# Two attention layers on one core: score tiles in three double banks, two of which are lent to the other products between groups of scores

## The chip, the core and the metric

The kernel runs on one core of a Trainium2 chip. The metric is the device time of one launch in microseconds; lower is better. The engines named here are TensorE (PE, matrix products; its weight loads have a row of their own, PEld), VectorE (DVE), ScalarE (ACT), GpSimd (POOL) and SyncE (SP, which issues DMAs). TensorE writes its results into PSUM, which this kernel divides into eight banks, each holding 512 fp32 values for every one of the 128 partitions. All data is fp32.

## The reference

Four images of 32x32 tokens and 768 channels go through two attention layers, each with a group norm before it and a residual around it.

```python
# layer 0 (12 heads of 64)
x = x + proj(softmax(q k^T / 8 + rel_h(q) + rel_w(q)) v)      # q, k, v = gn(x) @ W + b
# layer 1
q, k, v = layer_norm(dwconv3x3(gn(x) @ w_qkv.T + b_qkv))        # per head
x = x + proj(softmax(q k^T / 8 + rel_h(q) + rel_w(q)) v + q)
```

`rel_h` and `rel_w` are position biases that are made from q itself: one term for the key's row, one for the key's column. In layer 0 the bias of v can be added after the softmax, because the weights of the softmax sum to one.

## The kernel before

The work is cut into 8 stages (an image in a layer; images 0 and 1 in layer 0, the same two in layer 1, then images 2 and 3 in the same way), and each stage into 6 pairs of heads: 48 pairs in all. `attend` runs one pair. For each half of the queries (512, two halves) and for each group of four blocks of 128 keys it makes four score tiles, so there are 192 groups and 768 score tiles. A score tile is 128 keys by 2 heads by 512 queries and fills two banks. TensorE makes it from q and k (line 669) and adds the position bias (line 671); ACT takes its exponential into SBUF (line 676). After the four score tiles of a group come further products, then the four products with v (line 690), which add up in one bank, `av`; DVE adds the exponentials for the softmax's denominator (lines 682 and 684).

Everything else is woven in. `attend` yields four times per group, and each yield is a step; a table `events` says which pieces of other work are issued at which step: the q, k and v products of the next pair (`product`, `plain_v`, and in layer 0 `sevens`, which makes four products of halves out of seven), the convolution on DVE (`taps`), its layer norm (`centre`, `squares`, `norm`, `back`), the position products (`positions`), the group norm of the next stage, and the output projection of the last stage (`project`). The order on TensorE, DVE, ACT and GpSimd is the order in which the program issues; nothing reorders it. So an instruction that waits holds back all that follows on its engine.

Steps 0 and 1 stand between the first group's scores and its products with v, steps 2 and 3 after those products, steps 4 to 7 the same for the second group, steps 8 to 15 for the second half of the queries.

PSUM: `ps_s` holds two score tiles (four banks), `ps_av` one bank, and `ps_m` three banks, which all other products take in turn (`bank`). A tile can be written anew once the last reader of the tile that had its place is done. So the third score tile of a group waits for the exponential of the first, and the fourth for that of the second.

The softmax's denominator is finished late: `attend` leaves two pieces, `sums` (product `z`, line 639, and the reciprocal on ACT) and `result` (four instructions on DVE), in the list `rest`, and `more()`, called after the scores and after the products with v of each group, issues one of them.

In layer 0 the bias of v enters in `project`: for image 0, each of six output blocks gets six products of one column (`pbias`, line 713), which turn the bias of v into a bias of the output. Layer 1 does the same with the bias of its layer norm. `mix_tokens` (line 234) makes in five DVE instructions the sums of token halves that `sevens` reads.

Of the kernel before, what the change touches and what calls it, by code (L numbers as in the profile page):

```python
# [9 lines left out]
F32 = mybir.dt.float32  # L10
# [7 lines left out]
P = 128  # L18
# [7 lines left out]
QC = 512  # L26
# [19 lines left out]
def two_layers(ctx: ExitStack, tc: tile.TileContext, keep, x_in, wqkv, wproj, rels, windows, vrow, small, const, onehot, picks, out):  # L46
# [25 lines left out]
    work = pool("work", 2)  # L72
    one = pool("one", 1)
    stat = pool("stat", 3)
    ps_s = pool("ps_s", 2, space=PSUM)
    ps_av = pool("ps_av", 1, space=PSUM)
    ps_m = pool("ps_m", 3, space=PSUM)

    def bank(name):
        return ps_m.tile([P, 512], F32, tag="bank", name=name)  # L80

    def halves(ps, a, b, start=True, stop=True, **kw):

# [153 lines left out]
    def group_norm(stage):  # L237

        xn = xns[stage]
        st = stat.tile([P, NC * 2, 6], F32, tag="bn", name="bn", bufs=1)  # L240
        for n in range(NC):
            for h in range(2):
                nc.vector.bn_stats(st[:, 2 * n + h, :], xn[:, n, h * HALF : (h + 1) * HALF])
            if n in (1, 3):
                yield
        mv = stat.tile([P, 2], F32, tag="mv", name="mv")
        nc.vector.bn_aggr(mv, st.rearrange("p a b -> p (a b)"))
        yield
        yield
        group = cst[:, GROUP : GROUP + P]  # L250
        ps = bank("gn_mean")
        nc.tensor.matmul(ps[:, 0:1], group, mv[:, 0:1], start=True, stop=True)
        mean = stat.tile([P, 1], F32, tag="gmean", name="gmean")
        nc.vector.tensor_copy(mean, ps[:, 0:1])
        d = stat.tile([P, 1], F32, tag="gd", name="gd")
        nc.vector.tensor_sub(d, mv[:, 0:1], mean)
        nc.vector.scalar_tensor_tensor(d, d, d, mv[:, 1:2], ALU.mult, ALU.add)
        yield
        yield
        ps = bank("gn_var")  # L260
        nc.tensor.matmul(ps[:, 0:1], group, d, start=True, stop=True)
        v = stat.tile([P, 1], F32, tag="gv", name="gv")
        nc.vector.tensor_scalar(v, ps[:, 0:1], EPS, None, ALU.add)
        yield
        r = rsqrt(v, 1, "gn")
        yield
        for n in range(NC):
            nc.vector.tensor_scalar(xn[:, n, :], xn[:, n, :], mean, r, ALU.subtract, ALU.mult)  # L268
            if n % 2:
                yield  # L270
# [7 lines left out]
    sk = fixed.tile([P, NSMALL], F32, tag="sk", name="sk")  # L278
    nc.vector.tensor_scalar(sk, sm, SCALE, None, ALU.mult)

    pbias = fixed.tile([P, 2, NC], F32, tag="pbias", name="pbias")

    ones = fixed.tile([P, T], F32R, tag="ones", name="ones")
    plain = one.tile([P, T], F32, tag="whole", name="plain")
# [8 lines left out]
    class Pair:  # L293
# [15 lines left out]
        def sevens(self, s, second):  # L309

            xn = xns[self.b, self.layer]
            x11, x12, x21, x22 = (xn[:, n : n + 3, h : h + HALF] for n in (0, 3) for h in (0, HALF))

            def m(ps, at, x, more=False):

                w = weights[self.i, s, at // 2][:, 3 * (at % 2) : 3 * (at % 2) + 3, :]  # L320
                for t in range(4 if s else 1):
                    for n in range(3):
                        flags = dict(start=not (t or n or more), stop=n == 2, skip_group_check=True)
                        if s:
                            tokens = slice(t * P, (t + 1) * P)
                            halves(ps[:, tokens], x[:, n, tokens], w[:, n, :], **flags)
                        else:
                            halves(ps, w[:, n, :], x[:, n, :], **flags)

            add = lambda to, x, y, op=ALU.add: nc.vector.tensor_tensor(to, x, y, op)  # L330
            u, w = terms
            if not second:
                self.banks = b1, b2 = bank("m4m2"), bank("m3m5")
                m(b1, 0, x21)
                nc.scalar.copy(u, b1)
                m(b2, 1, x12)
                used((self.i, s, 0))
                add(u, u, b2)
                m(b1, 2, x11, more=True)
                add(w, u, b1, ALU.subtract)  # L340
                self.put(s, 1, 0, b1)
                m(b2, 3, x22, more=True)
                used((self.i, s, 1))
                add(u, u, b2, ALU.subtract)
                self.put(s, 0, 1, b2)
            else:
                b3, b4 = bank("m1m6"), bank("m7")
                m(b3, 4, quarters[0])
                add(u, u, b3)
                m(b4, 5, quarters[2])  # L350
                used((self.i, s, 2))
                self.put(s, 0, 0, b4, u)
                m(b3, 6, quarters[1], more=True)
                used((self.i, s, 3))
                self.put(s, 1, 1, b3, w)
# [258 lines left out]
    def attend(pair, os):  # L614
# [7 lines left out]
        def more():  # L622
            nonlocal found
            if rest:
                found = rest.pop(0)(*found)

        for c in range(T // QC):
# [6 lines left out]

            def sums(weighed, acc, c=c):

                z = bank("z")
                for j in range(2):
                    nc.tensor.matmul(  # L639
                        z[j * D : (j + 1) * D, :], cst[:, ONES : ONES + D], acc[:, j, :],  # L640
                        start=True, stop=True,
                    )
                at = 2 * (pair.i * (T // QC) + c)
                t = work.tile([P, QC], F32, tag="t", name="t", bufs=1)
                inv = work.tile([P, QC], F32, tag="inv", name="inv", bufs=1)
                nc.scalar.activation(t, z, AF.Copy, accum_out=seen[:, at : at + 1])

                nc.scalar.activation(inv, t, AF.Ln, bias=tiny)
                nc.scalar.activation(inv, inv, AF.Exp, scale=-1.0, accum_out=seen[:, at + 1 : at + 2])
                return weighed, t, inv  # L650

            def result(weighed, t, inv, cols=cols):

                nc.vector.scalar_tensor_tensor(t, t, -1.0, inv, ALU.mult, ALU.mult)
                nc.vector.scalar_tensor_tensor(inv, t, 2.0, inv, ALU.add, ALU.mult)

                if pair.layer:
                    nc.vector.tensor_tensor(inv, weighed, inv, ALU.mult)
                    nc.vector.scalar_tensor_tensor(q[:, cols], inv, col(LN + 4), q[:, cols], ALU.mult, ALU.add)
                else:  # L660
                    nc.vector.tensor_tensor(q[:, cols], weighed, inv, ALU.mult)

            for g in range(0, NKT, 4):
                es = []
                for kt in range(g, g + 4):
                    keys = slice(kt * P, (kt + 1) * P)
                    ps = ps_s.tile([P, 2, QC], F32, tag="s", name="s")
                    for j, rows in enumerate(heads):
                        nc.tensor.matmul(ps[:, j, :], k[rows, keys], q[rows, cols], start=True, stop=False)  # L669
                    for j, rows in enumerate(heads):  # L670
                        nc.tensor.matmul(  # L671
                            ps[:, j, :], ones[rows, keys], bias[c][rows, kt // 2, :],
                            start=False, stop=True,
                        )
                    e = work.tile([P, 2, QC], F32, tag="e", name="e", bufs=4)
                    nc.scalar.activation(e, ps, AF.Exp)  # L676
                    es.append(e)
                more()
                if g == 0:
                    av = ps_av.tile([P, QC], F32, tag="av", name="av")  # L680
# [6 lines left out]
                for t, e in enumerate(es):  # L687
                    kt = g + t
                    for j in range(2):
                        nc.tensor.matmul(  # L690
                            av[j * D : (j + 1) * D, :], pair.vt[:, kt, j * D : (j + 1) * D], e[:, j, :],
                            start=(kt == 0), stop=(kt == NKT - 1),
                        )
                more()
                if g + 4 == NKT:
                    rest.extend((sums, result))
                    found = (copy(av), acc)
                yield
                yield
# [1 line left out]
    def project(stage, os):  # L701
# [3 lines left out]
        for m in range(NC):  # L705
            w = wp.tile([P, NC, P], F32, tag="wproj", name="wproj_t")
            nc.sync.dma_start(w, wproj[layer, :, :, m, :].rearrange("h p q -> p h q"))
            bias = col(BIAS[layer] + 18 + m)
            if b == 0:
                ps = bank("pbias")  # L710
                for n in range(NC):
                    v_bias = col(LN + 5) if layer else col(BIAS[0] + 12 + n)
                    nc.tensor.matmul(ps[:, 0:1], w[:, n, :], v_bias, start=(n == 0), stop=(n == NC - 1))
                nc.vector.tensor_tensor(pbias[:, layer, m : m + 1], ps[:, 0:1], bias, ALU.add)
            bias = pbias[:, layer, m : m + 1]
            for h in range(2):
                cols = slice(h * HALF, (h + 1) * HALF)
                x = wp.tile([P, HALF], F32, tag="x", name="x")
# [16 lines left out]
    for k in range(1, len(stages)):  # L735
# [5 lines left out]
        if stages[k][1] == 0:  # L741
            mix = mix_tokens(stages[k])
            for r in range(5):
                at(first + 5 * n_steps + r - (0 if stages[k - 1][1] else 8), lambda mix=mix: next(mix, None))
        elif stages[k - 1][1] == 0:
            at(first + 4 * n_steps + 6, lambda: [nc.gpsimd.memset(pad, 0.0) for pad in pads])
    mix = mix_tokens(stages[0])
# [29 lines left out]
    def check():  # L777
# [2 lines left out]
        nc.vector.tensor_reduce(total, seen, AX.X, ALU.add)  # L780
        good = stat.tile([P, 1], F32, tag="good", name="good")
        nc.vector.tensor_scalar(good, total, LIMIT, None, ALU.is_lt)
        ps = bank("good")
        nc.tensor.matmul(ps[:1, :1], cst[:, ONES : ONES + 1], good, start=True, stop=True)
        bad = keep.tile([1, 1], mybir.dt.int32, tag="bad", name="bad")
        nc.vector.tensor_scalar(bad, ps[:1, :1], -1.0, 1.0 * P, ALU.mult, ALU.add)
# [5 lines left out]
    bad = check()  # L792
    for piece in last[2:]:
        piece()
    return bad
@with_exitstack
def general(ctx: ExitStack, tc: tile.TileContext, bad, x_in, wqkv, wproj, rels, windows, vrow, small, const, onehot, picks, out):
# [286 lines left out]
```

## Time and profile before

| what | value |
|---|---|
| median of 3 runs (lowest to highest) | 4041.1 us (4039.57 to 4045.22) |
| the profiled execution | 4040.44 us, its span 4038.7 us, granted TensorE clock 0.996 |
| busy: PE, PEld, DVE, ACT, POOL | 98%, 43%, 62%, 45%, 10% |
| chain that ended last, PE's share | 85% |
| PE's first matmul starts, last one ends | 15.3 us, 4032.9 us after the span's start |

Busy time of an engine counts from an instruction's start to its end as the profile models it. Matmuls overlap in the pipeline, so a busy TensorE can still be late: what a wait costs is read from the distance between starts. Waits are listed with the one that waited, what ended the wait, the sum in us, how often, and the longest.

### The profile page before, as it was taken

The numbers are of one execution on the slowest core, as the hardware profiler recorded it, in microseconds if no ns is written. First come the engines' busy times: TensorE is split into PE (matmuls) and PEld (weight loads), VectorE is DVE, ScalarE is ACT, GpSimd is POOL, SyncE is SP. The second block draws the span as 40 slices with busy tenths as digits, with TensorE's granted clock in tenths as the row PEclk, the third lists the DMA queues.
The fourth block names the chain that finished last, engine by engine and source line by source line (L and its number), as shares of the span: only waits on it lengthen the run. The fifth ranks groups of instructions, "written<-read, shape, count | busy, mean of one in ns | idle before, by whom it ended". The sixth has DMA issues, their size and how long they took to land.

```text
span 4038.7 us, 79929 instructions
## 1 busy us (share of the span) xinstructions
PE 3945.2 (98%) x35098; PEld 1720.3 (43%) x35098; DVE 2494.3 (62%) x2800; ACT 1812.1 (45%) x2669; POOL 409.8 (10%) x776
## 2 busy tenths in 40 slices
PE   7999999999999999999899999999999999999999
PEld 3534444434344444444444344354343444434443
DVE  2455423558489985799633454245575898848883
ACT  2444424545255553455423544244443555525552
POOL 0111100110000110010011110001100011000010
PEclk9999999999999999999999999999999999999999
DMA  5333242221411222212133222422114112131112
GB/s 160 85 112 113 71 128 73 57 65 38 132 48 38 76 52 75 63 49 69 41 103 88 58 70 63 144 58 70 47 53 127 37 43 53 40 104 43 38 47 75
DMA packets 179046, 293.34 MB, mean 73 GB/s; under 512 B 22528, under 2 KB 77952, under 8 KB 178688
## 3 DMA queue, kind: packets, MB, share of 16 engines
q1 hardware_dynamic: 117248, 187.41, 14.8%
q0 software_dynamic: 61440, 100.71, 10.9%
q8 instruction: 279, 4.57, 0.5%
q14 instruction: 79, 0.65, 0.1%
HBM read 153.36 MB, written 34.01 MB: 46 GB/s over the span
## 4 chain that ended last, share of the span: by engine, by line
PE 85%; DVE 8%; ACT 3%; issue 1%; DMA 1%; POOL 0%; DVEq 0%; SPq 0%; ACTq 0%
PE qkv L85 18%; PE av L690 14%; PE s L669 14%; PE proj L85 12%; PE m3m L85 4%; PE m4m L85 4%; PE m1m L85 4%; PE s L671 3%; PE ln_c L85 3%; PE rel L517 3%; PE z L639 2%; DVE shared L459 2%; DVE acc L684 2%; PE m L85 2%; ACT e L676 2%
## 5 line engine op out<-in xcount | busy, mean ns | idle before, releaser
L676 ACT ACTIVATE e<-s 128x1024 f32<-128x1024 f32 x768 | 781.3, 1023 | 529.8 <-PE s L671 503.7
L669 PE MATMUL s<-q,k 64*128 64x512 f32 x3072 | 831.8, 618 | 27.9 <-ACT e L676 22.2
L684 DVE TENSOR_TENSOR acc<-acc,e 128x1024 f32<-128x1024 f32 x576 | 705.4, 1225 | 184.4 <-ACT e L676 133.4
L85 PE MATMUL qkv<-xn,wqkv_t 128*64 128x512 f32 x3648 | 815.6, 596 | 2.8 <-DVE xn L268 2.6
L459 DVE SCALAR_TENSOR_TENSOR shared<-shared,sm 128x1056 f32<-128x1056 f32 x576 | 758.3, 1316 | 14.9
L671 PE MATMUL s<-bias,ones 64*128 64x512 f32 x1536 | 615.6, 794 | 13.9 <-DMA bias<-whole 9.5
L690 PE MATMUL av<-e,vt 128*64 128x512 f32 x2624 | 594.5, 595 | 0.0
L544 POOL DMA_DIRECT2D bias<-high x384 | 204.1, 552 | 3356.5 <-ACT high L533 3097.9
L85 PE MATMUL proj<-q,wproj_t 128*64 128x512 f32 x2304 | 504.9, 593 | 0.0
L85 PEld LDWEIGHTS qkv<-xn,wqkv_t 128*64 128x64 f32 x3648 | 252.9, 137 | 488.5 <-issue 482.6
L669 PEld LDWEIGHTS s<-q,k 64*128 64x128 f32 x3072 | 255.4, 186 | 362.0 <-ACT e L676 210.6
L442 ACT ACTIVATE shared<-qkv,sm 128x512 f32<-128x512 f32 (+1 forms) x288 | 129.2, 501 | 595.6 <-PE qkv L85 595.6
L723 DVE SCALAR_TENSOR_TENSOR x<-proj,pbias,x 128x512 f32<-128x512 f32 x96 | 72.1, 751 | 439.4 <-PE proj L85 435.0
L690 PEld LDWEIGHTS av<-e,vt 128*64 128x64 f32 x2624 | 184.7, 137 | 347.5 <-issue 328.9
L682 DVE TENSOR_TENSOR acc<-e 128x1024 f32<-128x1024 f32 x96 | 117.6, 1225 | 345.4 <-ACT e L676 344.6
L85 PEld LDWEIGHTS proj<-q,wproj_t 128*64 128x64 f32 x2304 | 163.7, 137 | 313.5 <-issue 311.7
L671 PEld LDWEIGHTS s<-bias,ones 64*128 64x128 f32 x1536 | 150.2, 188 | 199.6 <-issue 193.6
L544 POOL DMA_DIRECT2D bias<-whole x384 | 204.9, 562 | 119.5 <-DVE whole L534 109.0
L632 ACT COPY weighed<-av 128x512 f32<-128x512 f32 x96 | 56.3, 586 | 329.2 <-PE av L690 329.2
L85 PEld LDWEIGHTS ln_c<-cst,shared 128*64 128x64 f32 x2304 | 131.4, 138 | 44.4 <-issue 34.6
L517 PEld LDWEIGHTS rel<-q,rel 64*32 64x32 f32 x6144 | 111.6, 105 | 78.0 <-issue 61.0
L85 PE MATMUL ln_c<-cst,shared 128*64 128x128 f32 x2304 | 139.2, 274 | 3.1 <-DVE shared L459 3.1
(119 smaller groups left out, 3613.0 us busy)
## 6 DMA issues: line engine op xcount, KB each, us to landing
bias<-high POOLq DMA_DIRECT2D x384, 128.0 KB, 2.8
bias<-whole POOLq DMA_DIRECT2D x384, 128.0 KB, 3.0
wqkv_t<-in_wqkv SPq DMA_DIRECT2D x78, 384.0 KB, 3.1
wqkv_t<-mixed SPq DMA_DIRECT2D x66, 384.0 KB, 3.1
wproj_t<-in_wproj SPq DMA_DIRECT2D x48, 384.0 KB, 3.7
wqkv_t<-in_wqkv SPq DMA_DIRECT2D x66, 192.0 KB, 2.5
xn<-in_x SPq DMA_DIRECT2D x24, 512.0 KB, 7.8
x<-in_x SPq DMA_DIRECT2D x48, 256.0 KB, 2.8
```

The source lines that it names most:

```text
L85: nc.tensor.matmul(ps[lo : lo + D], a[:, lo : lo + D], b, start=start, stop=stop, **kw)
L442: nc.scalar.activation(self.pad[s][:, rows, there : there + src.shape[2]], src, AF.Identity, bias=col(self.column(s)))
L459: nc.vector.scalar_tensor_tensor(y, window, tap, y, ALU.mult, ALU.add)
L517: nc.tensor.matmul(ps[lo : lo + S, k * S : (k + 1) * S].rearrange("p (b c) -> p b c", b=2), rel[rows, 2 * self.layer + i, first : first + ...
L544: nc.gpsimd.dma_start(sets, some.unsqueeze(1).to_broadcast([D // 2, 2, QC]))
L639: nc.tensor.matmul(z[j * D : (j + 1) * D, :], cst[:, ONES : ONES + D], acc[:, j, :], start=True, stop=True,)
L669: nc.tensor.matmul(ps[:, j, :], k[rows, keys], q[rows, cols], start=True, stop=False)
L671: nc.tensor.matmul(ps[:, j, :], ones[rows, keys], bias[c][rows, kt // 2, :], start=False, stop=True,)
L676: nc.scalar.activation(e, ps, AF.Exp)
L682: nc.vector.tensor_tensor(acc, es[0], es[1], ALU.add)
L684: nc.vector.tensor_tensor(acc, acc, e, ALU.add)
L690: nc.tensor.matmul(av[j * D : (j + 1) * D, :], pair.vt[:, kt, j * D : (j + 1) * D], e[:, j, :], start=(kt == 0), stop=(kt == NKT - 1),)
```

## The change

- PSUM is divided otherwise. `ps_a` holds one score tile (two banks, bank 0 and 1), `ps_av` one bank, `ps_small` one bank, and two places, `place_b` and `place_c`, have two banks each. A place can be opened as a pair (one score tile) or as two single banks; each opening closes the pool that was there. The four score tiles of a group go to a, b, c and a.
- The other products take single banks: two from one place, then two from the other. `other_work` sets which place comes first: b after the scores, c after the products with v. `sevens` takes its banks from place c, and one from the small bank.
- The products `z`, `gn_mean`, `gn_var`, `pbias` and `good` go to the small bank.
- Layer 0's bias of v: the six times six products of one column are gone in layer 0 (36 matmuls, six DVE additions); the projection adds its own bias directly. Instead `result` leaves its quotient in `inv`, and a third piece, `finish`, lets ACT copy it into q with the bias of v added: one instruction of 128x512 for each pair and half of layer 0, 48 in all.
- `mix_tokens` for image 2 in layer 0 (the stage that follows a stage of layer 1): its five instructions are issued at steps 0, 0, 0, 1, 1 of the pair before, in place of 0, 1, 2, 3, 4.

```diff
-    ps_s = pool("ps_s", 2, space=PSUM)
+    ps_a = pool("ps_a", 1, space=PSUM)
     ps_av = pool("ps_av", 1, space=PSUM)
-    ps_m = pool("ps_m", 3, space=PSUM)
+    ps_small = pool("ps_small", 1, space=PSUM)
+    class Place:
+        def __init__(self, side):
+            self.side, self.pool, self.n = side, None, 0
+        def close(self):
+            if self.pool is not None:
+                self.pool.close()
+                self.pool = None
+        def open(self):
+            self.close()
+            self.pool = ExitStack()
+            self.n = 0
+            return self.pool.enter_context(
+                tc.tile_pool(name=f"ps_{self.side}", bufs=1, side=self.side, space=PSUM, reuse_waits="tile")
+            )
+        def pair(self, name):
+            return self.open().tile([P, 2, 512], F32, tag="pair", name=name)
+        def single(self, name):
+            if self.n % 2 == 0:
+                self.singles = self.open()
+            self.n += 1
+            return self.singles.tile([P, 512], F32, tag=f"single{self.n % 2}", name=name)
+    place_b, place_c = Place("left"), Place("right")
+    places = [place_b, place_c]
+    def other_work(first, second):
+        places[:] = [first, second]
+        first.n = second.n = 0
     def bank(name):
-        return ps_m.tile([P, 512], F32, tag="bank", name=name)
+        place = places[0]
+        ps = place.single(name)
+        if place.n % 2 == 0:
+            places.reverse()
+        return ps
+    def small_bank(name):
+        return ps_small.tile([P, 512], F32, tag="small", name=name)
...
-                self.banks = b1, b2 = bank("m4m2"), bank("m3m5")
+                place_c.n = 0
+                b1, b2 = place_c.single("m4m2"), place_c.single("m3m5")
...
-                b3, b4 = bank("m1m6"), bank("m7")
+                place_c.n = 0
+                b3, b4 = small_bank("m1m6"), place_c.single("m7")
+                place_c.n = 0
...
-                z = bank("z")
+                z = small_bank("z")
...
-                    nc.vector.tensor_tensor(q[:, cols], weighed, inv, ALU.mult)
+                    nc.vector.tensor_tensor(inv, weighed, inv, ALU.mult)
+                return (inv,)
+            def finish(inv, cols=cols):
+                if not pair.layer:
+                    nc.scalar.activation(q[:, cols], inv, AF.Identity, bias=col(pair.column(2)))
...
-                for kt in range(g, g + 4):
+                for kt, place in zip(range(g, g + 4), (None, place_b, place_c, None)):
-                    ps = ps_s.tile([P, 2, QC], F32, tag="s", name="s")
+                    ps = place.pair("s") if place else ps_a.tile([P, 2, 512], F32, tag="a", name="s")
...
+                other_work(place_b, place_c)
                 more()
...
+                other_work(place_c, place_b)
                 more()
                 if g + 4 == NKT:
-                    rest.extend((sums, result))
+                    rest.extend((sums, result, finish))
...
-            if b == 0:
-                ps = bank("pbias")
-                for n in range(NC):
-                    v_bias = col(LN + 5) if layer else col(BIAS[0] + 12 + n)
-                    nc.tensor.matmul(ps[:, 0:1], w[:, n, :], v_bias, start=(n == 0), stop=(n == NC - 1))
-                nc.vector.tensor_tensor(pbias[:, layer, m : m + 1], ps[:, 0:1], bias, ALU.add)
-            bias = pbias[:, layer, m : m + 1]
+            if layer:
+                if b == 0:
+                    ps = small_bank("pbias")
+                    for n in range(NC):
+                        nc.tensor.matmul(ps[:, 0:1], w[:, n, :], col(LN + 5), start=(n == 0), stop=(n == NC - 1))
+                    nc.vector.tensor_tensor(pbias[:, m : m + 1], ps[:, 0:1], bias, ALU.add)
+                bias = pbias[:, m : m + 1]
...
-                at(first + 5 * n_steps + r - (0 if stages[k - 1][1] else 8), lambda mix=mix: next(mix, None))
+                at(first + 5 * n_steps + (r // 3 if stages[k - 1][1] else r - 8), lambda mix=mix: next(mix, None))
```

More of the change, by code (lines that the diff above doesn't have):

```diff
@@ L250, in group_norm @@
         group = cst[:, GROUP : GROUP + P]
-        ps = bank("gn_mean")
+        ps = small_bank("gn_mean")
         nc.tensor.matmul(ps[:, 0:1], group, mv[:, 0:1], start=True, stop=True)
@@ L259, in group_norm @@
         yield
-        ps = bank("gn_var")
+        ps = small_bank("gn_var")
         nc.tensor.matmul(ps[:, 0:1], group, d, start=True, stop=True)
@@ L279, in two_layers @@
     nc.vector.tensor_scalar(sk, sm, SCALE, None, ALU.mult)
-    pbias = fixed.tile([P, 2, NC], F32, tag="pbias", name="pbias")
+    pbias = fixed.tile([P, NC], F32, tag="pbias", name="pbias")
     ones = fixed.tile([P, T], F32R, tag="ones", name="ones")
@@ L782, in check @@
         nc.vector.tensor_scalar(good, total, LIMIT, None, ALU.is_lt)
-        ps = bank("good")
+        ps = small_bank("good")
         nc.tensor.matmul(ps[:1, :1], cst[:, ONES : ONES + 1], good, start=True, stop=True)
@@ L794, in two_layers @@
         piece()
+    for place in (place_b, place_c):
+        place.close()
     return bad
```

## The prediction, made before the changed kernel was run

> **What bounds the kernel now.** I read the page's busy times first, then the waits of PE, then the timeline inside the score groups.
>
> ```profile
> PE 3945.2 (98%) x35098; PEld 1720.3 (43%) x35098; DVE 2494.3 (62%) x2800; ACT 1812.1 (45%) x2669; POOL 409.8 (10%) x776
> L676 ACT ACTIVATE e<-s 128x1024 f32<-128x1024 f32 x768 | 781.3, 1023 | 529.8 <-PE s L671 503.7
> L669 PE MATMUL s<-q,k 64*128 64x512 f32 x3072 | 831.8, 618 | 27.9 <-ACT e L676 22.2
> ```
>
> PE is the bound: 98% busy, and 85% of the chain that ended last. It waits for exponentials for only 22.2 us. The loads' waits tell more:
>
> ```profile
> PEld s L669 <- ACT e L676: 210.6, 383, 2.4
> PE s L669 <- ACT e L676: 22.2, 43, 1.8
> PE m4m L85 <- DVE xn L234: 5.9, 2, 5.5
> ```
>
> 383 is two for nearly each of the 192 groups: the third and fourth score tile wait for a free buffer. What that costs is seen in starts. A plain group (all timelines: start, duration, engine, instruction):
>
> ```profile
> 1361.40 1.13 PE L669 MATMUL s<-q,k 64*128 64x512 f32 x4
> 1362.10 0.61 ACT L473 COPY shared<-ln_c 128x512 f32<-128x512 f32 x1
> 1362.37 0.42 PEld L669 LDWEIGHTS s<-q,k 64*128 64x128 f32 x4 [0.23 <-issue]
> 1362.60 1.02 PE L669 MATMUL s<-q,k 64*128 64x512 f32 x4
> 1362.80 2.11 ACT L676 ACTIVATE e<-s 128x1024 f32<-128x1024 f32 x2
> 1363.88 0.30 PEld L669 LDWEIGHTS s<-q,k 64*128 64x128 f32 x4 [0.66 <-ACT e L676]
> 1363.88 1.13 PE L669 MATMUL s<-q,k 64*128 64x512 f32 x4
> 1364.96 0.31 PEld L669 LDWEIGHTS s<-q,k 64*128 64x128 f32 x4 [0.35 <-ACT e L676]
> 1365.08 1.02 PE L669 MATMUL s<-q,k 64*128 64x512 f32 x4
> ```
>
> The four tiles start 1.20, 1.28 and 1.20 us apart. Unhindered it is 1.193 us, with the load 0.23 ahead of its matmul. The third tile starts 0.06 after the first exponential ends, load and matmul together, and is 0.088 late. The fourth also waits, but its wait ends 0.17 before its turn and it loses nothing. These two cases price every wait below: released at least 0.17 before its turn, a tile loses nothing; released at R or later than its turn, it starts at R + 0.06. Behind a position product it is worse:
>
> ```profile
> 1400.11 1.13 PE L669 MATMUL s<-q,k 64*128 64x512 f32 x4
> 1400.22 0.58 ACT L522 COPY whole<-rel 64x512 f32<-64x512 f32 x1 [0.32 <-PE rel L517]
> 1400.81 1.01 ACT L523 COPY whole<-rel 64x512 f32<-64x512 f32 x1
> 1401.30 1.03 PE L669 MATMUL s<-q,k 64*128 64x512 f32 x4
> 1401.85 1.94 ACT L676 ACTIVATE e<-s 128x1024 f32<-128x1024 f32 x2
> 1402.93 1.13 PE L669 MATMUL s<-q,k 64*128 64x512 f32 x4 [0.36 <-ACT e L676]
> 1404.12 1.02 PE L669 MATMUL s<-q,k 64*128 64x512 f32 x4
> ```
>
> ACT's copies of `rel` push the first exponential back, and the third tile comes 1.63 after the second, 0.43 late.
>
> **What the Trainium skill says.** "PSUM — Partial Sum Buffer", Specifications (TRN2): eight banks of 512 fp32 values in a partition, so a third score buffer must take two banks from other products. The same page, Engine vs sequencer instructions: ACT's and DVE's queues are strictly in order; the trace agrees, the exponential at 1401.85 stands behind the copy. "TensorE: Matmul & The Clock Gate", Step-by-step: TensorE pulls weight loads ahead of running matmuls; here 1362.37 before 1362.60, and not where a semaphore holds (1363.88). "Perfetto Trace Analysis", Optimization Strategy: the same gap repeating on the engine that should be saturated can mean too little PSUM; here 0.088 us in every group at the least.
>
> **The change, part by part.** PE's order stays the same but for `pbias` of layer 0; SP's and POOL's orders stay. ACT gets `finish`; DVE loses six additions and moves the mixing.
>
> *Third score place.* I took the time from a group's first to last score matmul in all 192 groups of the trace, against 4.047 us without any lateness. Six groups hang on a DMA of the position bias (2 to 6 us each); I leave them as they are. For the others the program tells which instruction last reads the banks that each tile takes over, and the trace when that reader ends. PE and ACT order being kept, these times hold relative to the group's first tile.
> - The fourth tile (place a again) waits for the first exponential: due at 3.58, the exponential ends at 2.41 in a plain group, at most 3.3 in all but three. No loss. In those three (excess 1.82 now, the exponential queued behind a layer-norm Ln that waits for DVE) it ends at 4.16, and 0.64 is left.
> - The second tile takes place b, due at 1.193. In 18 groups b was last a `rel` bank, whose second copy ends at 1.72 to 1.76: late by 0.595 on average, against 0.439 now. In 24 groups it was `ln_c`, read by 1.298 (1362.10 + 0.61 above): late by 0.165, against 0.088. With a q/k/v product in b (18 groups) the reader ends at 1.015, 0.18 before its turn: no loss. A projection in b is read by 0.87.
> - The third tile takes c, due at 2.386; its latest reader ends at 1.76. No loss.
> - First product after the scores: its bank's exponential ended at least 0.86 before, in the present trace.
>
> Sum: 144 groups lose 29.0 us now and 1.9 after, gain 27.1; 24 groups 24 x (0.088 - 0.165) = -1.8; 18 groups 18 x (0.439 - 0.595) = -2.8. Net gain 22.4. In the three groups with 1.18 of gain the next `ln_c` waits for the convolution, which was done 0.82 before; 3 x 0.36 = 1.1 is given back. **21.3 us.**
>
> *pbias of layer 0.*
>
> ```profile
> L713 PE MATMUL pbias<-sm,wproj_t 128*128 128x1 f32 x144 | 18.0, 252 | 0.0
> ```
>
> 144 records are 12 blocks; each block sets PE back 1.43 us, start to next start. Six go: **8.6 us**, straight off PE. The six DVE additions (0.158 each) are not on the path.
>
> *finish.* 48 ACT instructions from SBUF to SBUF, with bias; such a row is `q<-shared,sm`, 0.721 us. 48 x 0.721 = 34.6 us on ACT, which is 45% busy. It is issued after the four exponentials of a half's second group, so copies and product readers behind it come 0.72 later, under products with v that take 3.4 us. The projection reads q only after those. Cost nothing; without cover 34.6 us.
>
> *Mixing.* PE waits 5.5 us for the fourth mixing instruction, which ends at 1966.88. Issued early, it follows the additions that end at 1957.1: four times 1.75 makes 1964.1, so the first product starts 2.8 earlier. But the softmax pieces (2.8) and four additions (5.1) now stand behind the fifth (1965.9), so the first sum that `sevens` needs comes at 1974.5, and the product on the same bank that started at 1976.35 starts about then. **1.8 us.**
>
> *Small bank, opening and closing.* `z`, group norm and `m1m6` find the bank's reader done over 1.5 us before, but for the start of the kernel. PE waits for itself 458 times instead of 365; the awaited matmul is five or more before. The trace has no such wait so near: at 0.06 from release to start, 93 more cost 5.6 us at most; a gain has no reason. I take nothing, since the awaited matmul ends about 1 us before the turn.
>
> Sum 21.3 + 8.6 + 1.8 = 31.7. Against the profiled 4040.4 (span 4038.7 and 1.7 around it) 4008.7; the median of the runs is 0.7 higher: **4009 us**.
>
> **Rivals.**
> 1. *Half the gain.* DVE is the reason that layer 1 can't go faster (it is 78% busy in 973 to 1990 us, PE 98%), and late readers hit more groups. For it: `ln_c` waits on the convolution with 0.82 to spare in places. Against it: layer 1's pairs hold 4.7 of the 22.4. If they give nothing (3.6 after the 1.1) and each opened place costs 0.03 us more (384 of them, 11.5), 15 us is lost: about 4024.
> 2. *Slower: the opened place exposes the weight loads.* The second and third tile of every group now wait for ACT where, before, the first two were free. If a wait keeps back the load although it has ended, each loses up to the load's lead of 0.23 us. At 0.15 it is 384 x 0.15 = 58: about 4067. It turns slower from (31.7 + 8.1) / 384 = 0.10 a tile on. Against it: the fourth tile has such a wait today and keeps its 1.193.
> 3. *Nothing changes.* The waits for exponentials are already cover for something else and only move; with pbias alone and as much given back at place b: about 4038. Against it: the second tile is late in 42 groups only.
> 4. *More.* Products before waiting tiles, too, gain from the fourth single bank: about 3997.
>
> **How the numbers follow.** My forecast has 0.70 (own range 4002 to 4017), rival 1 0.13, rival 2 0.08, rival 3 0.06, rival 4 0.03. The measurement of this kernel tells 0.2%, 8.1 us, from no change, so faster means under 4033. Faster: 0.70 + 0.13 + 0.03 = 0.86; same 0.06; slower 0.08. The range 3999 to 4032 takes in the forecast, the bounds of the near self-waits and rival 1.
>
> **What would show it.** Right: the third tile of a group at 1.193 after the second; the second tile waiting for `whole` L523 in about 18 groups and `ln_c` L473 in about 24, in layer 1; 72 `pbias` records; the wait for `xn` L234 gone down to about 3 us. Wrong: second or third tiles with load and matmul starting together although their reader had ended (rival 2); waits of PE on DVE in layer 1 that grow by more than 5 us (rival 1); `finish` ending waits of PE.

## The result, and the profile after

The changed kernel takes 3979.28 us (median of 4 runs, 3978.31 to 3982.59) against 4043.16 (4 runs, 4039.57 to 4045.98): 0.9844 of the time, 95% interval 0.9827 to 0.9861. That is 64 us less, where 32 were forecast. The sign was right; the time lies below the range of 3999 to 4032. In the profiled executions the span fell from 4038.7 to 3977.6 us, by 61.1, at the same clock of 0.996. The page of the kernel after: busy times, the first two groups that answer to those shown of before, and the shares of the chain that ended last.

```profile
PE 3898.5 (98%) x35026; PEld 1736.9 (44%) x35026; DVE 2492.3 (63%) x2794; ACT 1840.8 (46%) x2717; POOL 411.5 (10%) x776
...
PE 90%; DVE 6%; DMA 2%; issue 1%; ACT 1%; POOL 0%; DVEq 0%; SPq 0%; ACTq 0%
...
L731 ACT ACTIVATE e<-s 128x1024 f32<-128x1024 f32 x768 | 780.7, 1025 | 470.6 <-PE s L726 437.4
L724 PE MATMUL s<-q,k 64*128 64x512 f32 x3072 | 817.3, 608 | 11.1 <-ACT whole L572 7.6
```

PE's share of the span is still 98%, but its busy time is 46.7 us less, while its idle time (span less busy) is only 14.4 less. So most of what was won had stood in the records as *busy* PE. About 9 us of it are the `pbias` products that are gone; the records of the score tiles alone cover 39.0 us less (947.9 before, 908.9 after). The mean product of q and k went from 618 to 608 ns although its work is the same. The waits of PE of the kernel after (engine, product and line, what it waited for: total, times, longest, in us):

```profile
PE ln_c L131 <- DVE shared L508: 6.2, 2, 3.9
PE s L724 <- ACT whole L572: 7.6, 18, 0.4
PE s L724 <- ACT e L731: 2.7, 3, 0.9
```

The wait for exponentials is down from 22.2 us to 2.7; the new one, for the copies of `rel` that hold place b, comes 18 times. Now a plain group of the kernel after on the timeline (start, duration, engine, instruction):

```profile
1347.84 0.30 PEld L724 LDWEIGHTS s<-q,k 64*128 64x128 f32 x4 [0.81 <-issue]
1347.84 1.13 PE L724 MATMUL s<-q,k 64*128 64x512 f32 x4
...
1348.80 0.42 PEld L724 LDWEIGHTS s<-q,k 64*128 64x128 f32 x4 [0.23 <-ACT ln_ln L153]
1349.04 1.02 PE L724 MATMUL s<-q,k 64*128 64x512 f32 x4
...
1349.89 0.42 PEld L724 LDWEIGHTS s<-q,k 64*128 64x128 f32 x4 [0.24 <-issue]
1350.12 1.02 PE L724 MATMUL s<-q,k 64*128 64x512 f32 x4
...
1350.98 0.42 PEld L724 LDWEIGHTS s<-q,k 64*128 64x128 f32 x4 [0.24 <-issue]
1351.21 1.02 PE L724 MATMUL s<-q,k 64*128 64x512 f32 x4
```

The tiles start 1.20, 1.08 and 1.09 us apart. Where a load runs 0.23 us ahead of its product, the products last 1.02 us and the next tile can start 1.085 after. Where load and product start together, as at 1347.84, they last 1.13 and the next tile starts 1.193 after. The difference of 0.108 us is what an *exposed load* costs, that is, one that doesn't run ahead. The first tile of a group always has one, in both kernels, so 1.193, which the forecast took for the unhindered distance, was the distance behind an exposed load.

The group behind a position product, and the one that the prediction showed as plain (its first ACT lines are the readers of `ln_c`), after the change:

```profile
1372.64 1.13 PE L724 MATMUL s<-q,k 64*128 64x512 f32 x4
1372.76 0.58 ACT L571 COPY whole<-rel 64x512 f32<-64x512 f32 x1 [0.32 <-PE rel L566]
1373.35 1.02 ACT L572 COPY whole<-rel 64x512 f32<-64x512 f32 x1
1374.42 1.13 PE L724 MATMUL s<-q,k 64*128 64x512 f32 x4 [0.41 <-ACT whole L572]
1375.61 1.02 PE L724 MATMUL s<-q,k 64*128 64x512 f32 x4
1376.70 1.02 PE L724 MATMUL s<-q,k 64*128 64x512 f32 x4
```

```profile
1334.29 1.13 PE L724 MATMUL s<-q,k 64*128 64x512 f32 x4
1334.98 0.60 ACT L522 COPY shared<-ln_c 128x512 f32<-128x512 f32 x1
1335.64 0.30 PEld L724 LDWEIGHTS s<-q,k 64*128 64x128 f32 x4 [0.62 <-ACT shared L522]
1335.64 1.13 PE L724 MATMUL s<-q,k 64*128 64x512 f32 x4
1336.84 1.02 PE L724 MATMUL s<-q,k 64*128 64x512 f32 x4
1337.92 1.02 PE L724 MATMUL s<-q,k 64*128 64x512 f32 x4
```

In both the *second* tile is late, as forecast, and it too then runs 1.13 and puts the third off by a further 0.11.

Summed over all 192 groups, from the start of the first to the start of the last score product of each, the trace gives:

| groups, by what the kernel after shows | number | before, us | after, us | difference of the unrounded sums |
|---|---|---|---|---|
| second tile not late | 138 | 581.1 | 528.8 | -52.3 |
| second tile behind `ln_c` | 24 | 99.3 | 98.2 | -1.0 |
| second tile behind `rel` | 18 | 80.7 | 81.5 | +0.7 |
| others (bias DMAs, late exponentials, stretches at a lower clock) | 12 | 75.5 | 73.0 | -2.5 |
| all | 192 | 836.6 | 781.5 | -55.1 |

The 138 groups are of two kinds before. In 116 the tiles are as far apart as in the plain group; in 22 the first exponential is later and the third tile comes 1.63 us after the second. After the change both kinds take some 3.83 us.

Of the 61.1 us, 55.1 are in the scores. The six `pbias` blocks that are gone were priced at 8.6; by that price the rest of the program is 2.6 longer. One wait in it is some 3 us longer: that of `ln_c` for the convolution, behind one of the groups counted as others (0.9 before, 3.9 after). That group took 2.3 us more before than after, in a stretch (3912 to 3919 us) in which the granted clock was 0.76. The longer wait offsets what it shows as won.

### The profile page after: what moved, and what is told of

Read it like the earlier page. It is cut to its first block, busy times and chain, and to the rows that moved or that the text cites. A ratio compares the mean times of both kernels' runs of the same rounds, so it can differ in the third digit from the quotient of the medians.

```text
span 3977.6 us, 79975 instructions
## 1 busy us (share of the span) xinstructions
PE 3898.5 (98%) x35026; PEld 1736.9 (44%) x35026; DVE 2492.3 (63%) x2794; ACT 1840.8 (46%) x2717; POOL 411.5 (10%) x776
## 4 chain that ended last, share of the span: by engine, by line
PE 90%; DVE 6%; DMA 2%; issue 1%; ACT 1%; POOL 0%; DVEq 0%; SPq 0%; ACTq 0%
PE qkv L131 19%; PE s L724 15%; PE av L746 15%; PE proj L131 13%; PE m3m L131 4%; PE m4m L131 4%; PE s L726 4%; PE m1m L131 4%; PE ln_c L131 3%; PE rel L566 3%; PE z L688 2%; PE m L131 2%; DVE shared L508 2%; DVE acc L740 2%; PE ln_t L544 1%
## 5 line engine op out<-in xcount | busy, mean ns | idle before, releaser
L724 PE MATMUL s<-q,k 64*128 64x512 f32 x3072 | 817.3, 608 | 11.1 <-ACT whole L572 7.6
L724 PEld LDWEIGHTS s<-q,k 64*128 64x128 f32 x3072 | 277.7, 187 | 281.1 <-issue 203.9
L780 DVE SCALAR_TENSOR_TENSOR x<-proj,sm,x 128x512 f32<-128x512 f32 x48 | 36.1, 751 | 217.4 <-PE proj L131 213.1
L780 DVE SCALAR_TENSOR_TENSOR x<-proj,pbias,x 128x512 f32<-128x512 f32 x48 | 36.0, 750 | 216.1 <-PE proj L131 211.7
```

## The experiments

**Theory A**, from the two traces: an unhindered tile takes 1.085 us. A tile whose bank is released too late loses the wait and, since its load is then exposed, 0.108 more. The third tile of a plain group of before lost 1.280 - 1.085 = 0.195 and 0.108, together 0.303, not 0.088. Two rivals stand beside it in the expectations: that the PSUM places are worth about the forecast's 21 us and the rest comes from elsewhere in the change, and that the gain comes from the third place or the fourth single bank as such, and not from the tile that was late. The kernel before, run beside the experiments, had medians of 4042.55 to 4043.35.

### The PSUM places alone

The changed kernel, with the v bias and the mixing as they were before:

```diff
-                    rest.extend((sums, result, finish))
+                    rest.extend((sums, result))
...
-            if layer:
-                if b == 0:
+            if b == 0:
...
-                at(first + 5 * n_steps + (r // 3 if stages[k - 1][1] else r - 8), lambda mix=mix: next(mix, None))
+                at(first + 5 * n_steps + r - (0 if stages[k - 1][1] else 8), lambda mix=mix: next(mix, None))
```

> The changed kernel with layer 0's bias of v and the mixing as before: the new division of PSUM alone. Theory A (a tile whose weight load had to wait for a semaphore runs 0.108 us longer, so the third score tile lost 0.195 + 0.108 in every group, and the prediction priced it at 0.088): nearly all of the 64 us comes from here, 3988 us (3983 to 3993), 55 below before. Rival B (the banks brought the 22 us of the prediction and the rest came from the bias of v or the mixing): 4021 us.

Measured: 3989.06 us (3986.55 to 3993.18), ratio 0.9867 (0.9852 to 0.9883), so 53 us less than before. The score groups sum to 782.7 us, as in the full change. The places alone bring the unexpected part.

### The v bias by ACT alone

The kernel before, with `finish` and without layer 0's `pbias`, and nothing else.

```diff
-                    nc.vector.tensor_tensor(q[:, cols], weighed, inv, ALU.mult)
+                    nc.vector.tensor_tensor(inv, weighed, inv, ALU.mult)
...
-                    rest.extend((sums, result))
+                    rest.extend((sums, result, finish))
...
-            if b == 0:
+            if layer:
+                if b == 0:
```

> The kernel before with the bias of v of layer 0 added by ACT and without its 36 products of one column: that part alone. Theory A: 8.6 us less than before, as six blocks of 1.43 us go, so 4034 us. Rival B: 30 us or more, under 4015. Rival C (the copy on ACT, 48 times 0.72, lands on the path): 4043 or more.

Measured: 4032.32 us (4030.29 to 4033.33), ratio 0.9973 (0.9961 to 0.9984), so 10 us less. As in the changed kernel, 72 `pbias` products are left:

```profile
L719 PE MATMUL pbias<-sm,wproj_t 128*128 128x1 f32 x72 | 9.0, 251 | 0.0
```

The forecast of 8.6 for this part lies inside the interval (6 to 16 us).

### The mixing steps alone

The kernel before, with one line of the change.

```diff
-                at(first + 5 * n_steps + r - (0 if stages[k - 1][1] else 8), lambda mix=mix: next(mix, None))
+                at(first + 5 * n_steps + (r // 3 if stages[k - 1][1] else r - 8), lambda mix=mix: next(mix, None))
```

> The kernel before with the mixing for image 2 at steps 0, 0, 0, 1, 1: that part alone. Theory A: 2 us less, 4041 us, within what can be told from no change; in the profile the wait of PE for xn (5.5 us at its longest) is under 3.5 or gone, and the two sums after it wait longer. Rival B: 10 us or more less.

Measured: 4038.21 us (4036.15 to 4042.37), ratio 0.9990 (0.9982 to 0.9999): 4 us less, with an interval that nearly reaches nothing and holds the forecast 1.8. The wait for `xn` at `m4m` went from 5.9 us to 3.0:

```profile
PE m4m L85 <- DVE xn L234: 3.0, 2, 2.7
```

The three parts alone add up to 53.5 + 10.2 + 4.3 = 68 us, against 64 for the whole: with intervals of several us on each, the measurement doesn't tell whether the parts help or hinder each other.

### Early release, without a third place

This keeps before's two buffers and makes the third and fourth tile's banks free sooner: for the first two tiles of a group ACT reads only one of the two banks. The exponential of the second head's scores is left out there, so this kernel serves for timing alone.

```diff
-                    nc.scalar.activation(e, ps, AF.Exp)
+                    if kt % 4 < 2:
+                        nc.scalar.activation(e[:, 0, :], ps[:, 0, :], AF.Exp)
+                        nc.scalar.activation(e[:, 1, :], e[:, 0, :], AF.Identity)
+                    else:
+                        nc.scalar.activation(e, ps, AF.Exp)
```

> The kernel before, its PSUM as it was, but in the first two tiles of each group the exponential reads one of the two banks and the other half of its output is a copy of the first half: the exponential of the second head's scores is left out there. The tile is released after 0.59 us in place of 1.02; ACT works 0.17 us longer for each. Theory A (the lateness of the third tile is all that the two buffers cost, wait plus exposed load): the starts of a plain group go from 1.193, 1.280, 1.193 to 1.193, 1.085, 1.085; 144 groups x 0.30 = 43 us less, 4000 us (3993 to 4012). Prediction's price (0.088 a group, tiles at 1.193): 4020 us. Rival D (tiles follow each other faster only because each has a place of its own in PSUM): distances stay at 1.19, 4026 us or more.

Measured: 3989.00 us (3987.70 to 3991.25), ratio 0.9867 (0.9852 to 0.9883). That is the time of the PSUM places alone, without any third place. A group of this kernel on PE:

```profile
1355.79 1.13 PE L669 MATMUL s<-q,k 64*128 64x512 f32 x4
...
1356.98 1.03 PE L669 MATMUL s<-q,k 64*128 64x512 f32 x4
...
1358.06 1.03 PE L669 MATMUL s<-q,k 64*128 64x512 f32 x4
...
1359.16 1.02 PE L669 MATMUL s<-q,k 64*128 64x512 f32 x4
```

The third tile starts 1.08 after the second, and the score groups sum to 783.1 us. So neither a third place nor the fourth single bank nor the new order of the other products is needed for a gain of this size: an earlier release does it. That the two times agree to 0.1 us is chance, though. The 138 groups gain 44.0 us here, against 52.3 in the full change, because 21 of them still have a late third tile. Behind `ln_c` and `rel` the second tile has a buffer of its own and isn't late; these 42 groups gain 13.8, against 0.3. The others lose 4.4. Theory A's middle value, 11 us higher, had counted plain groups only.

### The third tile late again, with three places

```diff
-                for kt, place in zip(range(g, g + 4), (None, place_b, place_c, None)):
+                for kt, place in zip(range(g, g + 4), (None, place_b, None, place_c)):
```

The changed kernel, with the third tile in place a (behind the first exponential) and the fourth in c.

> The changed kernel with the score tiles in places a, b, a, c: still three places, but the third tile waits for the first exponential again, and the fourth is free. Theory A: in a plain group the starts are 1.193, 1.280, 1.193 (the fourth has no wait, yet comes 0.108 later because the third ran with its load exposed), so 0.30 in 144 groups and 0.1 in the others: 61 us more than the changed kernel, 4040 us (4028 to 4046). Rival D (the distance is short because each tile has a place of its own): the fourth comes 1.085 after the third, 4008 us.

Measured: 4036.50 us (4034.34 to 4041.37), ratio 0.9984 (0.9977 to 0.9991). All the rest of the change is in, and 57 us are gone again. The loads' waits of this kernel:

```profile
PEld s L724 <- ACT e L731: 128.4, 192, 2.4
```

One load in each of the 192 groups waits for an exponential, and the score groups sum to 839.2 us. The expected total was nearly met, but not by its own terms, which add up to 48 and not 61: in the 22 groups with the later exponential the third tile comes 1.63 after the second again, and not 1.28. The change's gain is a matter of *which* tile takes the place again, not of how many places there are.

### The fourth tile late

```diff
-                for kt, place in zip(range(g, g + 4), (None, place_b, place_c, None)):
+                for kt, place in zip(range(g, g + 4), (None, place_b, place_c, place_b)):
```

> The changed kernel with the score tiles in places a, b, c, b: the fourth tile waits for the second exponential. Theory A: that one ends about 3.53 after the group's first start, the fourth is due at 3.36, so it is 0.22 late and runs 0.108 longer, which now falls on the block after it; in all 192 groups, with the late second tiles on top: 70 us more, 4049 us (4035 to 4058). If an exposed load costs nothing on the last tile: 4029 us.

Measured: 4110.04 us (4107.54 to 4112.02), ratio 1.0167 (1.0151 to 1.0182): 131 us more than the changed kernel. Both expectations missed it. The score groups sum to 839.6 us, which is 58 more and what a late tile in each group costs by the other runs. The waits of PE name most of the rest; some 13 us were not traced further:

```profile
PE qkv L131 <- ACT e L731: 55.1, 50, 1.1
...
PE proj L131 <- ACT e L731: 3.4, 3, 1.1
PE rel L566 <- ACT e L731: 1.1, 1, 1.1
```

Other products stand in place b right after the scores, and place b now holds the fourth tile. A group's fourth tile and what follows it:

```profile
1389.45 0.30 PEld L724 LDWEIGHTS s<-q,k 64*128 64x128 f32 x4 [0.66 <-ACT e L731]
1389.45 1.13 PE L724 MATMUL s<-q,k 64*128 64x512 f32 x4
...
1390.74 1.08 PE L688 MATMUL z<-acc,cst 128*64 128x512 f32 x4
1390.85 1.02 ACT L731 ACTIVATE e<-s 128x1024 f32<-128x1024 f32 x1 [0.36 <-PE s L726]
...
1391.93 0.63 PEld L131 LDWEIGHTS ln_c<-cst,shared 128*64 128x64 f32 x12 [0.99 <-ACT e L731]
```

The load of `ln_c` waits until the fourth exponential ends at 1391.87, and starts 0.06 later.

This is repaired by the order of the other products alone:

```diff
-                other_work(place_b, place_c)
+                other_work(place_c, place_b)
                 more()
...
-                other_work(place_c, place_b)
+                other_work(place_b, place_c)
                 more()
```

> The run with places a, b, c, b for the four tiles, changed in one point: the first product after the scores takes place c (whose exponential, the third, ended long before) and the first one after the products with v takes place b. Theory A says that the 131 us of that run are two things: the fourth tile late by 0.303 in each group, since it waits for the second exponential (192 x 0.303 = 58), and the products right behind the scores, which stood in place b and waited for the fourth exponential (60 of idle PE by the waits, and their exposed loads). The second goes away, the first stays: 3979 + 58 = about 4037 (4024 to 4052, since which product was last in place b, and so which second tile is late, changes too). If instead the products behind the scores wait on ACT whatever bank they have, or the fourth tile's wait alone cost the 131: 4095 to 4115.

Measured: 4031.70 us (4029.44 to 4035.41), ratio 0.9972 (0.9961 to 0.9983), inside the expected range. 78 of the 131 us go, and the 55.1 us of waits of `qkv` for exponentials with them; the score groups sum to 842.6 us, as late as before. A late tile thus costs about the same whether it is the third or the fourth (57 and 52 us above the changed kernel). Letting the next product take a place whose exponential is still to come costs 78 us, more than the whole change gained.

### The second tile in the place not used last

The changed kernel, with the second tile in whichever of b and c the other products used longer ago, and the third in the other one; the other products keep their order relative to these.

```diff
         def single(self, name):
...
+            used_last[0] = self
...
-                for kt, place in zip(range(g, g + 4), (None, place_b, place_c, None)):
+                early, late = (place_c, place_b) if used_last[0] is place_b else (place_b, place_c)
+                for kt, place in zip(range(g, g + 4), (None, early, late, None)):
...
-                other_work(place_b, place_c)
+                other_work(early, late)
...
-                other_work(place_c, place_b)
+                other_work(late, early)
```

> The changed kernel with one more rule: the second score tile takes the place that other work did not use last, the third the other one; the places for other work follow. So the second tile no longer waits for the copies of rel (18 groups, 0.583 + 0.108 each) or of ln_c (24 groups, 0.165 + 0.108 each), and the third is due late enough for both. Theory A: 18 x 0.69 + 24 x 0.27 = 19 us less than the changed kernel, 3960 us (3955 to 3968). Without the exposed load: 3965. If the waits only move on to the third tile or to the products after the scores: 3979.

Measured: 3963.73 us (3961.12 to 3967.95), ratio to before 0.9807 (0.9793 to 0.9820), 16 us below the changed kernel. No PE wait for `whole` is left, and the group behind a position product runs as a plain one:

```profile
1368.01 1.13 PE L727 MATMUL s<-q,k 64*128 64x512 f32 x4
1368.12 0.58 ACT L573 COPY whole<-rel 64x512 f32<-64x512 f32 x1 [0.32 <-PE rel L568]
...
1368.71 1.02 ACT L574 COPY whole<-rel 64x512 f32<-64x512 f32 x1
...
1369.20 1.02 PE L727 MATMUL s<-q,k 64*128 64x512 f32 x4
...
1370.29 1.02 PE L727 MATMUL s<-q,k 64*128 64x512 f32 x4
...
1371.37 1.02 PE L727 MATMUL s<-q,k 64*128 64x512 f32 x4
```

The 24 groups behind `ln_c` give 6.3 us and the 18 behind `rel` 12.6 in the trace; 1.5 comes back in the others. The score groups sum to 764.1 us. By time alone this run doesn't tell the waits with the exposed load from the waits without. The trace does: the expectation's terms for the two kinds are 6.5 and 12.4 us with the exposed load, and 4.0 and 10.5 without; and in these groups the third tile is 1.085 after the second here, and 1.19 in the changed kernel. This version beats both kernels.

## Why the prediction was right or wrong

**The step that failed is one sentence: "Unhindered it is 1.193 us".** It was taken from the first distance in a group of before, 1.20, and it agreed with the third. But both of these stand behind a tile whose load and product start together. The load 0.23 ahead that the sentence names is the second tile's own, and shows in the distance after that tile, not before it. The page's figures to see it were in the fence that the prediction showed: 1.13 at 1361.40 and 1363.88, 1.02 at 1362.60 and 1365.08. The rule made from it, that a tile released late starts 0.06 us after its release, was right for that tile and left out the next: the late tile lasts 0.108 longer. So of 1.280 between second and third tile 0.195 was lost, not 0.088, and the fourth tile, said to lose nothing, lost 0.108. In the sum this is the term "144 groups lose 29.0 us now and 1.9 after, gain 27.1". For the 138 of them in the table it can be set beside the trace: before, they lie 22.6 us above the forecast's 4.047 a group, and that is all that it could win back there. They gained 52.3. The missing 29.7 is the baseline: without lateness such a group takes 3.831 us, which is 0.216, or twice 0.108, below 4.047; and 138 x 0.216 = 29.8.

Why it didn't show in the waits: PE's idle time for exponentials was 22.2 us. The Trainium skill, "Perfetto Trace Analysis", Tensor Engine Instruction, says that the end of a TensorE record is estimated from the instruction's size and not observed. That fits here: the scores took 55.1 us less from start to start, and 39.0 of that was booked as busy time, so the idle time could not show it. The prediction rightly read starts, but compared them with the wrong one.

**The other terms.**
- The 24 `ln_c` groups: the second tile was to be 0.165 late, and is 1.349 - 1.193 = 0.156. The groups gained 1.0 us instead of losing 1.8.
- The `rel` groups: due at 1.193 + 0.595 = 1.788, found at 1.774 as a median, 18 waits for `whole` as forecast. The groups are 0.7 us up where 2.8 was said. Both kinds came out some 0.11 us a group better than forecast: their fourth tile now comes some 1.09 after the third, where the forecast took 1.193.
- The three groups with the exponential queued behind a layer-norm Ln: 5.87 before, 4.99 after in each, 0.87 gained where 1.18 was said. The `ln_c` behind each then waits 0.24 for DVE, 0.7 in all where 1.1 was to be given back. (The wait of 3.9 named above stands elsewhere.)
- `pbias`: 8.6 forecast, 10 alone, not to be told apart; 72 records, as said. `finish` ends no wait of PE.
- Mixing: 1.8 forecast, 4 alone with an interval of 0.4 to 7.3. In the changed kernel the wait for `xn` is missing from the list of waits, but only its name has changed. It now stands here, as the longest of four:

```profile
PE m4m L131 <- issue: 4.6, 4, 3.0
```

  This product starts at 1933.64 us, 0.10 after the fourth mixing instruction ends. In the kernel with the PSUM places alone, where the mixing is as before, the same wait is 5.9 and is called "issue" too. So it fell by 2.8 (5.9 to 3.0), as forecast; what was to be given back later was not traced.
- The small bank and the opened places cost nothing that the traces show.

**The rivals.** Rival 1, half the gain, named the convolution, and one wait for it did grow, by some 3 us; the sign that it gave was more than 5. Rival 2, that each opened place exposes its load, is refuted by the plain group: loads at 1348.80 and 1349.89 run 0.23 ahead although both tiles have a bank that another engine had read. The change *removes* exposed loads: in the traces, 382 of before's 768 score tiles start load and product together, and 237 of after's. Rival 3 is refuted. Rival 4, more, was nearest in time (3997), but not for its reason: the early release gives the same gain without a fourth single bank.

**The range** of 3999 to 4032 took in the forecast, the near self-waits and rival 1; rival 4's 3997 lay just outside it. Every one of these cases used the same baseline, and none allowed for its being wrong. The price of a wait was taken as certain from two examples, both measured against a distance that had an exposed load in it.

## What to carry to other kernels

Before a wait on a saturated engine is priced, find one stretch where nothing waits and take its distance between starts as the baseline; if no stretch is free of waits, the shortest *record* of the operation (here 1.02 against 1.13 us) hints at it. A late release cost TensorE twice here: once for the wait, and once more since the weight load could no longer run ahead. When banks are lent to several users, let the user with the tightest turn take the bank whose last reader is longest gone: that alone was worth 16 us here, and giving the next product a bank whose reader had yet to run cost 78. And when a wait vanishes from a list, look at the place where it stood: it may have changed its name only.

## What the runs showed of the hardware

- A score tile (four records of 64x512 for q and k, two for the bias) starts 1.085 us after the one before if that one's load ran ahead, and 1.193 after if it started with its product. The Trainium skill, "TensorE: Matmul & The Clock Gate", Step-by-step, says that loads are pulled ahead of running matmuls; its price when this fails, 0.108 us here, was the surprise.
- The price goes by how far the load runs ahead (its lead). These figures are of tiles whose follower was not held up. In the kernel with places a, b, a, c, 25 third tiles have a lead of only 0.06 to 0.08 us; the lead and the distance to the next tile add up to 1.193 to 1.200 us in each. Over all ten traces, 76 tiles with a lead of 0.11 to 0.18 are followed after 1.089 us (median), 1400 with a longer one after 1.087, and some 2000 without a lead after 1.194. So each bit of lead saves as much, until the 0.108 are gone.
- The first score tile of a group, behind products with v, `ln_c` or `rel`, has an exposed load in every one of the 192 groups of every kernel run here. What keeps that load back was not tried. An estimate of its cost is 192 x 0.108, some 21 us.
